# A CIN kernel's opening: table copies, queue assignments and a turn in two halves

## Chip, cores and metric

The kernel runs on one NeuronCore of a Trainium2 chip. The metric is the device time of one execution in microseconds (us). "PE" is TensorE, "DVE" VectorE, "ACT" ScalarE, "POOL" GpSimd and "SP" SyncE. Times inside an execution are counted from the start of the profiled span.

## The reference

Three layers of a compressed interaction network (CIN) over x of shape 1024 x 39 x 64 (batch, fields, embedding), all in float32:

```python
def _cin_layer(Xk, X0, W, b):
    O = W.shape[0]
    Hk, Fdim = (Xk.shape[1], X0.shape[1])
    Wr = W.reshape(O, Hk, Fdim)
    return jnp.einsum('bhe,bfe,ohf->boe', Xk, X0, Wr) + b[None, :, None]
X0 = sparse_embedding
Xk = X0
outs = []
for W, b in ((W0, b0), (W1, b1), (W2, b2)):
    Xk = _cin_layer(Xk, X0, W, b)
    outs.append(Xk.sum(axis=-1))
cin_output = jnp.concatenate(outs, axis=-1)
return cin_output @ fc_w.T + fc_b
```

W0 is 64 x 1521, W1 and W2 are 64 x 2496, fc_w is 1 x 192; the output is 1024 x 1.

## The kernel before

**The main loop.** Products of pairs of fields are formed once and multiplied by weights. The batch is cut into 32 blocks of 2048 columns (32 samples of 64). For each block, tables `r` (four tiles of 128 rows), and for each pair of blocks `u` and `v`, hold fields of x gathered row by row from DRAM, so that each elementwise product of two table tiles on DVE (L163, L165) covers 128 pairs of fields. PE multiplies each product tile by a weight tile `wa` in four quarters of 512 columns into PSUM `po` (L489). A pair of blocks has 13 products: six for each block and one, of `u` and `v`, that both share. ACT and DVE finish a block (L508, L514, L519), and at the end one row of PE matmuls makes the output.

**The tables' way.** `load(n)` (L117, L119) writes block n's x, fields first, into a DRAM tile `xd`: 312 KB in pieces of 256 B. There are three such tiles, for two blocks each, with one more row of ones behind each block's 39 fields. `gather_rows` (L124, L125) is an indirect DMA on POOL's queue: it fetches a tile's 128 rows by a list of row numbers (`lists`). For block 0 alone there are two smaller DRAM tiles `xh`, one for each half of its columns, so that its first gathers can start early: x goes there by ACT's queue (L204) and the ones by SP's (L201). `xd[0]` is filled for both blocks by two loads on POOL's queue, load(1) behind six of block 0's gathers and load(0) behind the last (L285, L288). `roll_half(0)` gathers `u` and `v`, `roll(1)` block 1's four tables.

**The head**, before the first matmul of the loop, makes the weights. In the order of PE's program:

- `spin` (L229): matmuls of zeros that only keep PE running; the tile `zeros` is set by DVE (L189). Two of them, then `small` (L296) from the copies of fcrow on POOL (L276), then two more.
- L316: W2, weighted by `fc2` (L299), into `pv`; L294: five small turns of fc rows; L331: twenty transposes of W0's two halves `w0s` into `pw`.
- DVE (L337, L344) and ACT (L345) make V2 (`v2`) from `pv`. After one spin, L386 and L392 multiply W1 by V2: `w1s` holds W1's lower and upper half of columns in two groups of 64 partitions, which arrive by SP's queue (L202) and ACT's (L208).
- The result T lies in `pt` (fields 0 to 31) and `pv` (the last seven). DVE and ACT copy it into `part` (L407, one half of the columns of each field by each) and `rest` (L401). PE then turns it: `turn_fields` (L412), eight transposes of rows 64.. into `pw[1]`, eight of rows 0.. into `pw[0]`, four of `rest` into `pt[0]`; and three spins.
- `untwine` (L373) copies from `pw` and `pt` into the tile `both`; `pairs` (set to zero on POOL, L214) receives sums of elements of `both` (`weight_rows`, L438 on DVE, L442 on ACT); PE turns a weight tile (L473), ACT copies it to `wa` (L474), and L489 begins.

Each engine executes its instructions in the order of the program, and each DMA queue belongs to the engine that issues it. A tile framework adds the waits: for data, for buffers, and for a DMA that takes over the completion semaphore of an earlier one, of which there are eight for SP and ACT together and eight for POOL. That last kind is why, before the change, ACT's issue of W1's upper half (L208) waits for W2's arrival, and its issue of `xh[1]` for that of fcrow.

Of the kernel before, what the change touches and what calls it, by code (L numbers as in the profile page):

```python
# [54 lines left out]
F32 = mybir.dt.float32  # L55
# [5 lines left out]
B, F, E, H = 1024, 39, 64, 64  # L61
FH = F * H
# [12 lines left out]
MM = 512  # L75
SUB = 1024
BLK = 2048
NA = 16
NR = F - 2 * NA
NW = 20  # L80
# [3 lines left out]
FT = F + 1  # L84
# [14 lines left out]
def cin_kernel(ctx: ExitStack, tc: tile.TileContext, x, w0t, b0, w1, b1, w2, b2, fc_w, fc_b, out):  # L99
    nc = tc.nc  # L100
# [10 lines left out]
    xd = [dram.tile([2 * FT, BLK], F32, name=f"xd{k}") for k in range(NTAB)]  # L111
    xh = [dram.tile([FT, SUB], F32, name=f"xh{k}") for k in range(2)]

    def bank(name):
        return psum.tile([128, MM], F32, name=name, tag="po")

    def load(n, engine=nc.sync):  # L117
        first = n % 2 * FT
        engine.dma_start(  # L119
            xd[n // 2 % NTAB][first : first + F].rearrange("f (b e) -> f b e", e=E),  # L120
            xv[:, n * BB : (n + 1) * BB, :],
        )

    def gather_rows(dst, table, k):  # L124
        nc.gpsimd.indirect_dma_start(  # L125
            dst, None, table, bass.IndirectOffsetOnAxis(ap=lists[:, k : k + 1], axis=0)
        )
# [21 lines left out]
    rt = [const.tile([128, 4, BLK], F32, name=f"r{k}") for k in range(2)]  # L149
# [3 lines left out]
    both = const.tile([128, F * FT], F32, name="both")  # L153
    pairs = const.tile([128, NCHUNK, 128], F32, name="pairs")
# [13 lines left out]
    prep = tc.tile_pool(name="prep", bufs=1)  # L168
    with prep as prep:
        w2s = prep.tile([128, FH // 2], F32, name="w2s")  # L170
        w1s = prep.tile([128, FH // 2], F32, name="w1s")
        w0s = prep.tile([128, NW * H], F32, name="w0s")
        part = prep.tile([128, NA, H], F32, name="part")
# [2 lines left out]
        fcrow2 = prep.tile([1, H, 2], F32, name="fcrow2")  # L176
        fc2 = prep.tile([128, H], F32, name="fc2")
        ones = prep.tile([16, 2, 128], F32, name="ones")
        zeros = prep.tile([128, MM // 2], F32, name="zeros")
        warm = prep.tile([1, 1], F32, name="warm")  # L180
        place = prep.tile([128, 1], I32, name="place")
        apart = prep.tile([128, 128], I32, name="apart")
# [3 lines left out]

        nc.vector.memset(zeros, 0.0)  # L189
        nc.vector.memset(ones, 1.0)  # L190
        nc.vector.memset(fc2, 0.0)
        nc.vector.memset(v2, 0.0)
        nc.vector.memset(warm, 0.0)

        w0v = w0t.rearrange("b a h -> b (a h)")
        nc.sync.dma_start(fcrow, fc_w)
        nc.scalar.dma_start(w2s, w2.rearrange("o (s n) -> (o s) n", s=2))
        for s, n in enumerate((NW, F - NW)):
            nc.scalar.dma_start(w0s[H * s : H * s + F, 0 : n * H], w0v[:, s * NW * H : (s * NW + n) * H])
        for k in range(2):  # L200
            nc.sync.dma_start(xh[k][F:FT].rearrange("r (p c) -> p r c", c=128), ones[0:8, 0:1])  # L201
        nc.sync.dma_start(w1s[0:H], w1[:, 0 : FH // 2])  # L202
        for k in range(2):
            nc.scalar.dma_start(  # L204
                xh[k][0:F].rearrange("f (b e) -> b f e", e=E), x[k * SB : (k + 1) * SB]
# [4 lines left out]
        for i in range(3):  # L210
            for k, by in enumerate((STEP[i + 1], BASE[i + 1], EXTRA[i + 1] - K)):
                nc.gpsimd.memset(shifts[:, k, i : i + 1], float(by))
        nc.gpsimd.iota(apart, pattern=[[1, 128]], base=0, channel_multiplier=-1)
        nc.gpsimd.memset(pairs, 0.0)  # L214
        bothv = both.rearrange("p (a b) -> p a b", b=FT)
        nc.gpsimd.memset(bothv[0:H, :, F], 0.0)
        nc.scalar.copy(warm, warm)


# [1 line left out]
        pt = [bank("pt") for _ in range(2)]  # L221
        idle = bank("idle")
        pw = [bank("pw") for _ in range(2)]
        small = bank("small")


        def spin(n=1):
            for _ in range(n):
                nc.tensor.matmul(idle[:, 0 : MM // 2], zeros[:, 0:128], zeros, start=True, stop=True)  # L229

        spin(2)


        tmp = prep.tile([128, 16], F32, name="tmp")
# [5 lines left out]
        def new():  # L240
            used[0] += 1
            return tmp[:, used[0] - 1 : used[0]]

        def step(x, at, by, out=None):

            out = new() if out is None else out
            nc.vector.tensor_scalar(out, x, at, by, ALU.is_ge, ALU.mult)
            return out
# [4 lines left out]
        row, f0, j, extra, t, half, q = new(), new(), new(), new(), new(), new(), new()  # L253
# [21 lines left out]
        for s in range(2):  # L275
            nc.gpsimd.tensor_copy(fcrow2[:, :, s], fcrow[:, 2 * H : 3 * H])  # L276

        for k in range(NTAB):
            nc.gpsimd.dma_start(xd[k][F::FT].rearrange("r (p c) -> p r c", c=128), ones)

        halves = [slice(0, SUB), slice(SUB, BLK)]
        for k, cols in enumerate(halves):
            for i in range(3):
                gather_rows(rt[0][:, i, cols], xh[k], i)
        load(1, nc.gpsimd)  # L285
        for k, cols in enumerate(halves):
            gather_rows(rt[0][:, 3, cols], xh[k], 3)
        load(0, nc.gpsimd)  # L288


        one = ones[0:1, 0, 0:1]
# [6 lines left out]
        )  # L298
        nc.vector.tensor_scalar(fc2[:, 0::32], mask, small[:, 0:1], None, ALU.mult)  # L299
        nc.vector.tensor_scalar(unit, apart, 0, None, ALU.is_equal)  # L300
        spin(2)


        step(row, HR, 1.0, half)
        fused(q, half, -float(HR), row, ALU.mult, ALU.add)
        nc.vector.tensor_tensor(field[4], q, step(q, F, -float(F)), ALU.add)
        nc.vector.tensor_tensor(field[4], field[4], step(q, 56, 11.0), ALU.add)

# [4 lines left out]
        for k in range(2):  # L313
            for u in range(4):
# [5 lines left out]
                    start=True,  # L320
                    stop=True,
# [6 lines left out]
        for s in range(2):  # L328
            for k in range(NW // 2):
                n = min(128, (F - NW * s) * H - k * 128)  # L330
# [33 lines left out]
        copies = (nc.vector.tensor_copy, nc.scalar.copy)  # L364
# [24 lines left out]
        for s in range(2):  # L389
            rows = slice(H * s, H * s + H)  # L390
            for k in range(2):
# [4 lines left out]
                    start=True,  # L396
                    stop=True,
                )
        for s, copy in enumerate(copies):
            at = slice(32 * s, 32 * s + 32)  # L400
# [1 line left out]
                rest[:, :, at],  # L402
                pv[s][H * s : H * s + H, 0 : 32 * NR].rearrange("b (a h) -> b a h", h=32),
            )
        for s, copy in enumerate(copies):
            at = slice(32 * s, 32 * s + 32)
            copy(part[:, :, at], pt[s].rearrange("b (a h) -> b a h", h=32))  # L407

        def turn_fields(to, src, rows, n):
            for a in range(0, n, 2):  # L410
                m = min(2, n - a)
                nc.tensor.transpose(  # L412
                    to[0 : m * H, a // 2 * FT : a // 2 * FT + FT],
                    src[rows, a : a + m, :].rearrange("b a h -> b (a h)"),
                    unit[rows, rows],
                )

        spin()
        for k in (1, 0):
            turn_fields(pw[k], part, slice(H * k, H * k + FT), NA)  # L420
        turn_fields(pt[0], rest, slice(0, FT), NR)
        for k in (1, 0):
            untwine(copies[k], 1, NA * k, NA, NA // 2, pw[k], FT)
# [133 lines left out]
    p = {}  # L557
# [14 lines left out]
    n, c = steps[3]  # L572
# [8 lines left out]
    for at, (n, c) in enumerate(steps[:-TAIL]):  # L581
# [17 lines left out]
        if at + AHEAD < len(steps):  # L599
            n, c = steps[at + AHEAD]  # L600
# [70 lines left out]
```

## Time and profile before

| | |
|---|---|
| five runs | 750.69, 751.57, 752.64, 753.55, 753.83 us; median 752.64 |
| the profiled execution | 751.6 us of its own; span 749.8 us |
| PE busy in the span | 741.3 us (99%), of which L489 722.5 us |
| DVE, ACT, POOL busy | 643.2, 164.2, 318.7 us |
| first L489 | 22.1 us |
| half clock of PE | about 20.5 to 23.9 us |
| DMA | 180.40 MB, mean 241 GB/s |

A row of the groups reads: line, engine, operation, output <- inputs, shapes, count, then busy us and mean ns of one, then the idle time of the engine just before these instructions and what ended most of it. An idle time that ends on "remote" or on an unknown queue has a releaser that the profile could not name. Matmul ends are modelled, not observed. A float32 matmul is two passes, so the 896 matmuls of the loop stand as x1792.

### The profile page before, as it was taken

To read this page: it belongs to the slowest core of one execution; us is meant where nothing else is said; L and a number is where in the kernel's file an instruction comes from. 1 tells how busy PE (TensorE), PEld (TensorE's weight loads), DVE (VectorE), ACT (ScalarE), POOL (GpSimd) and SP (SyncE) were. 2 spreads that over 40 slices of the span, in tenths; PEclk is the share of its full clock that TensorE was granted. 3 is DMA by queue.
4 is the path that set the end of the run, shared out by engine and by line. 5 is a ranking of instruction groups with operands and counts; after the bars stand their busy time and mean duration, and the time that the engine had idled before them with its cause. 6 is when DMAs were issued, how large, how long until landed. Compare 5 with 4: busy or idle time off the path is not lost.

```text
span 749.8 us, 5288 instructions
## 1 busy us (share of the span) xinstructions
PE 741.3 (99%) x1911; PEld 324.0 (43%) x1911; DVE 643.2 (86%) x509; ACT 164.2 (22%) x224; POOL 318.7 (43%) x198
## 2 busy tenths in 40 slices
PE   8899999999999999999999999999999999999998
PEld 4444444444444444444444444444444444444443
DVE  4989899888889888899888899888899888898885
ACT  2122212221212222112221212222112221212222
POOL 6568633436243263532436243263532436343100
PEclk9999999999999999999999999999999999999999
DMA  7789976865757876565866757776575855747400
GB/s 230 255 304 382 375 303 202 336 244 201 289 174 281 259 278 246 184 275 205 336 235 213 272 183 287 259 273 238 191 284 204 336 224 180 271 148 299 168 1 0
DMA packets 59050, 180.40 MB, mean 241 GB/s; under 512 B 37164, under 2 KB 37229, under 8 KB 39056
## 3 DMA queue, kind: packets, MB, share of 16 engines
q0 software_dynamic: 24512, 169.76, 59.9%
q1 hardware_dynamic: 32902, 8.64, 5.1%
q10 hardware_dynamic: 1610, 1.67, 0.8%
q8 instruction: 15, 0.25, 0.1%
q14 instruction: 11, 0.09, 0.0%
HBM read 179.98 MB, written 10.60 MB: 254 GB/s over the span
## 4 chain that ended last, share of the span: by engine, by line
PE 99%; ACT 0%; another core or an unknown queue 0%; DVE 0%; issue 0%; ACTq 0%
PE po L489 96%; PE idle L229 1%; PE pt L392 0%; PE pv L316 0%; PE pt L412 0%; PE pw L331 0%; PE tr L473 0%; PE pw L412 0%; ACT both L373 0%; DVE g L528 0%; DVE sums L530 0%; ACT zq L527 0%; ACT part L407 0%; PE pv L386 0%
## 5 line engine op out<-in xcount | busy, mean ns | idle before, releaser
L489 PE MATMUL po<-p,wa 128*128 128x512 f32 (+1 forms) x1792 | 722.5, 595 | 0.0
L163 DVE TENSOR_TENSOR p<-r 128x2048 f32<-128x2048 f32 (+2 forms) x196 | 434.7, 2246 | 85.8 <-PE po L489 81.8
L489 PEld LDWEIGHTS po<-p,wa 128*128 128x128 f32 (+1 forms) x1792 | 313.7, 190 | 405.1 <-issue 384.9
L125 POOL DMA_INDIRECT r<-xd,lists x124 | 246.6, 1989 | 354.9 <-DVE p L163 334.2
L508 ACT ACTIVATE z<-po,fc0s 64x512 f32<-64x512 f32 x124 | 84.7, 683 | 354.2 <-PE po L489 347.3
L502 ACT COPY g<-u 39x1024 f32<-39x1024 f32 x64 | 66.6, 1043 | 184.5 <-DVE sums L519 184.3
L514 DVE SCALAR_TENSOR_TENSOR g<-po,b0s,z 64x512 f32<-64x512 f32 x124 | 86.4, 734 | 0.0
L519 DVE TENSOR_REDUCE sums<-g 103x16 f32<-103x1024 f32 x62 | 75.6, 1220 | 2.1
L125 POOL DMA_INDIRECT u<-xd,lists x16 | 34.1, 2131 | 11.5 <-DVE p L163 6.9
L165 DVE TENSOR_TENSOR p<-u,v 128x2048 f32<-128x2048 f32 x16 | 36.5, 2284 | 0.0
L125 POOL DMA_INDIRECT v<-xd,lists x16 | 17.7, 1109 | 4.9 <-issue 4.9
L125 POOL DMA_INDIRECT r<-xh,lists x8 | 7.7, 963 | 6.6 <-DVE v L344 4.5
L229 PE MATMUL idle<-zeros 128*128 128x256 f32 x20 | 8.2, 538 | 1.2 <-DVE zeros L189 1.2
L528 DVE SCALAR_TENSOR_TENSOR g<-po,b0s,zq 64x512 f32<-64x512 f32 x4 | 3.0, 743 | 5.3 <-ACT zq L527 5.3
L119 POOL DMA_DIRECT2D xd<-in_x x6 | 6.3, 1070 | 0.0
L373 DVE COPY both<-pw 64x390 f32<-64x390 f32 (+1 forms) x4 | 2.1, 523 | 4.8 <-remote 4.7
L229 PEld LDWEIGHTS idle<-zeros 128*128 128x128 f32 x20 | 4.6, 259 | 3.6 <-issue 1.8
L473 PE MATMUL tr<-unit,pairs 128*128 128x128 f32 x7 | 2.1, 305 | 4.0 <-ACT pairs L442 4.0
L474 ACT COPY wa<-tr 128x128 f32<-128x128 f32 x7 | 1.9, 266 | 19.1 <-PE tr L473 19.1
L438 DVE TENSOR_TENSOR pairs<-both 128x6 f32<-128x6 f32 (+27 forms) x50 | 5.4, 178 | 0.3 <-DVE both L373 0.3
L527 ACT ACTIVATE zq<-po,fc0s 64x512 f32<-64x512 f32 x4 | 2.7, 684 | 10.2 <-PE po L489 10.2
L473 PEld LDWEIGHTS tr<-unit,pairs 128*128 128x128 f32 x7 | 1.1, 161 | 6.1 <-ACT pairs L442 4.3
(92 smaller groups left out, 46.4 us busy)
## 6 DMA issues: line engine op xcount, KB each, us to landing
xd<-in_x SPq DMA_DIRECT2D x26, 312.0 KB
r<-xd,lists POOLq DMA_INDIRECT x124
xd<-in_x POOLq DMA_DIRECT2D x6, 312.0 KB
w2s<-in_w ACTq DMA_DIRECT2D x1, 624.0 KB
w1s<-in_w SPq DMA_DIRECT2D x1, 312.0 KB
xh<-in_x ACTq DMA_DIRECT2D x2, 156.0 KB
w1s<-in_w ACTq DMA_DIRECT2D x1, 312.0 KB
u<-xd,lists POOLq DMA_INDIRECT x16
```

The source lines that it names most:

```text
L119: engine.dma_start(xd[n // 2 % NTAB][first : first + F].rearrange("f (b e) -> f b e", e=E), xv[:, n * BB : (n + 1) * BB, :],)
L125: nc.gpsimd.indirect_dma_start(dst, None, table, bass.IndirectOffsetOnAxis(ap=lists[:, k : k + 1], axis=0))
L163: nc.vector.tensor_tensor(p[:, cols], r[:, i, cols], r[:, k, cols], ALU.mult)
L165: nc.vector.tensor_tensor(p, ut[n // 2 % 2], vt[n // 2 % 2], ALU.mult)
L229: nc.tensor.matmul(idle[:, 0 : MM // 2], zeros[:, 0:128], zeros, start=True, stop=True)
L438: nc.vector.tensor_tensor(out, diagonal(a, b, sa, sb), diagonal(b, a, sb, sa), ALU.add)
L473: nc.tensor.transpose(tr[:, at], pairs[:, c], unit)
L489: nc.tensor.matmul(po[n + h][m], wa[w, c, :], p[w, bass.ts(m, MM)], start=c == opens[n + h], stop=c == closes[n + h],)
L502: nc.scalar.copy(gt[H : H + F], ut[n // 2 % 2][h : h + F, bass.ts(m, SUB)])
L508: nc.scalar.activation(z[m // 2][:, bass.ts(m % 2, MM)], po[n][m][H:128], AF.Identity, bias=fc0s[H:128])
L514: nc.vector.scalar_tensor_tensor(gt[0:H, at], po[n][m][0:H], b0s, z[m // 2][:, at], ALU.add, ALU.mult)
L519: nc.vector.tensor_reduce(sums[:, b_at : b_at + SB], gt.rearrange("p (b e) -> p b e", e=E), AX.X, ALU.add)
```

## The change

Five edits, all ahead of the main loop.

1. `spin` reads a built-in constant of 1.0, broadcast, so the tile `zeros` and its memset go. There are three spins at first instead of two, and behind `small` one of 256 and one of 128 columns instead of two of 256.
2. The ones of `xh` are written by POOL's queue, ahead of `apart`, instead of SP's; the memsets of `pairs` and of a column of `both` move on POOL from ahead of the mask and the fcrow copies to behind them.
3. W1's lower half still goes by SP's queue, but waits for a memset of one of its columns that DVE executes behind the lists' work; W1's upper half stays where it was on ACT's queue.
4. Block 0's rows in `xd[0]` are copied from `xh[0]` and `xh[1]` (39 rows of 4 KB each) by SP's queue instead of loaded from x by POOL's; load(1) goes by SP's queue behind them.
5. T is copied to `part` in two halves of the fields by each of DVE and ACT, and turned in the order rows 64.., rows 0.. for the first half of the fields, then again for the second.

With this, completion semaphores are dealt out anew: ACT's issue of W1's upper half waits for none, and that of `xh[1]` for W2's arrival. The gathers of block 0 stand one behind the other on POOL, with no load between.

```diff
-        zeros = prep.tile([128, MM // 2], F32, name="zeros")
...
-        nc.vector.memset(zeros, 0.0)
         nc.vector.memset(ones, 1.0)
...
-        for k in range(2):
-            nc.sync.dma_start(xh[k][F:FT].rearrange("r (p c) -> p r c", c=128), ones[0:8, 0:1])
-        nc.sync.dma_start(w1s[0:H], w1[:, 0 : FH // 2])
...
+        for k in range(2):
+            nc.gpsimd.dma_start(xh[k][F:FT].rearrange("r (p c) -> p r c", c=128), ones[0:8, 0:1])
         nc.gpsimd.iota(apart, pattern=[[1, 128]], base=0, channel_multiplier=-1)
-        nc.gpsimd.memset(pairs, 0.0)
-        bothv = both.rearrange("p (a b) -> p a b", b=FT)
-        nc.gpsimd.memset(bothv[0:H, :, F], 0.0)
...
-        def spin(n=1):
+        def spin(n=1, cols=MM // 2):
             for _ in range(n):
-                nc.tensor.matmul(idle[:, 0 : MM // 2], zeros[:, 0:128], zeros, start=True, stop=True)
-
-        spin(2)
+                nc.tensor.matmul(
+                    idle[:, 0:cols],
+                    nc.const_aps.tensor(1.0, (128, 128), F32),
+                    nc.const_aps.tensor(1.0, (128, cols), F32),
+                    start=True,
+                    stop=True,
+                )
+
+        spin(3)
...
+        nc.gpsimd.memset(pairs, 0.0)
+        bothv = both.rearrange("p (a b) -> p a b", b=FT)
+        nc.gpsimd.memset(bothv[0:H, :, F], 0.0)
         for k in range(NTAB):
             nc.gpsimd.dma_start(xd[k][F::FT].rearrange("r (p c) -> p r c", c=128), ones)
-
-        halves = [slice(0, SUB), slice(SUB, BLK)]
-        for k, cols in enumerate(halves):
-            for i in range(3):
-                gather_rows(rt[0][:, i, cols], xh[k], i)
-        load(1, nc.gpsimd)
-        for k, cols in enumerate(halves):
-            gather_rows(rt[0][:, 3, cols], xh[k], 3)
-        load(0, nc.gpsimd)
...
-        spin(2)
+        spin()
+        spin(1, MM // 4)
...
+        nc.vector.memset(w1s[0:H, 0:1], 0.0)
+        nc.sync.dma_start(w1s[0:H], w1[:, 0 : FH // 2])
+
+        halves = [slice(0, SUB), slice(SUB, BLK)]
+        for k, cols in enumerate(halves):
+            for i in range(3):
+                gather_rows(rt[0][:, i, cols], xh[k], i)
+        for k, cols in enumerate(halves):
+            gather_rows(rt[0][:, 3, cols], xh[k], 3)
+            nc.sync.dma_start(xd[0][0:F, cols], xh[k][0:F])
+        load(1)
...
-        for s, copy in enumerate(copies):
-            at = slice(32 * s, 32 * s + 32)
-            copy(part[:, :, at], pt[s].rearrange("b (a h) -> b a h", h=32))
-
-        def turn_fields(to, src, rows, n):
-            for a in range(0, n, 2):
+        for q in range(2):
+            for s, copy in enumerate(copies):
+                fields = slice(q * NA // 2, (q + 1) * NA // 2)
+                copy(
+                    part[:, fields, 32 * s : 32 * s + 32],
+                    pt[s].rearrange("b (a h) -> b a h", h=32)[:, fields],
+                )
+
+        def turn_fields(to, src, rows, n, start=0):
+            for a in range(start, n, 2):
...
-        for k in (1, 0):
-            turn_fields(pw[k], part, slice(H * k, H * k + FT), NA)
+        for q in range(2):
+            for k in (1, 0):
+                rows = slice(H * k, H * k + FT)
+                turn_fields(pw[k], part, rows, (q + 1) * NA // 2, q * NA // 2)
```

More of the change, by code (lines that the diff above doesn't have):

```diff
@@ L198, in cin_kernel @@
         for s, n in enumerate((NW, F - NW)):
-            nc.scalar.dma_start(w0s[H * s : H * s + F, 0 : n * H], w0v[:, s * NW * H : (s * NW + n) * H])
-        for k in range(2):
-            nc.sync.dma_start(xh[k][F:FT].rearrange("r (p c) -> p r c", c=128), ones[0:8, 0:1])
-        nc.sync.dma_start(w1s[0:H], w1[:, 0 : FH // 2])
+            nc.scalar.dma_start(
+                w0s[H * s : H * s + F, 0 : n * H], w0v[:, s * NW * H : (s * NW + n) * H]
+            )
         for k in range(2):
@@ L404, in cin_kernel @@
             )
-        for s, copy in enumerate(copies):
-            at = slice(32 * s, 32 * s + 32)
-            copy(part[:, :, at], pt[s].rearrange("b (a h) -> b a h", h=32))
-        def turn_fields(to, src, rows, n):
-            for a in range(0, n, 2):
+        for q in range(2):
[4 more added lines that the diff above has]
+                    pt[s].rearrange("b (a h) -> b a h", h=32)[:, fields],
+                )
+        def turn_fields(to, src, rows, n, start=0):
+            for a in range(start, n, 2):
                 m = min(2, n - a)
```

## The prediction

> **What bounds the kernel now.** I read the page first, then the chain of waits, then the timeline of the first 50 us, then the table by stage. The page says that TensorE is never without work once the main loop runs:
>
> ```profile
> PE 741.3 (99%) x1911; PEld 324.0 (43%) x1911; DVE 643.2 (86%) x509; ACT 164.2 (22%) x224; POOL 318.7 (43%) x198
> ...
> PE 99%; ACT 0%; another core or an unknown queue 0%; DVE 0%; issue 0%; ACTq 0%
> ...
> L489 PE MATMUL po<-p,wa 128*128 128x512 f32 (+1 forms) x1792 | 722.5, 595 | 0.0
> ```
>
> The last line is the main matmul: 722.5 us busy, 0.0 us idle before it. Nothing in the diff touches L489, its operands or its count, so the change can move only what lies before the first of them (22.1 us), or starve them later. The chain of waits shows what that head is made of (start us, us, what):
>
> ```profile
> 9.86 0.63 PE idle L229 x2
> 10.49 0.54 PE pv L386 x2
> ...
> 14.33 0.97 PE pw L412 x16
> 15.29 1.31 PE pt L412 x4
> ...
> 17.49 2.03 another core or an unknown queue
> ...
> 20.98 0.45 PE tr L473
> 21.43 0.85 PE idle L229 x2
> 22.28 1.71 PE po L489 x2
> ```
>
> W2 by fc (L316), W0's turns (L331), W1 by V2 (L386, L392), the copies of T (L407), T's turns (L412), copies into `both` (L373), weight rows (L438), one turn (L473), first matmul. The 2.03 us of an unknown queue are put in their place by the timeline (start, us, engine line, then the idle time ahead and what ended it):
>
> ```profile
> 16.63 0.86 ACT L373 COPY both<-pw 64x320 f32<-64x320 f32 x2 [2.35 <-PE pt L412]
> 18.81 0.99 DVE L373 COPY both<-pw 64x320 f32<-64x320 f32 x2 [4.74 <-remote]
> 19.54 0.55 ACT L373 COPY both<-pt 64x160 f32<-64x160 f32 x2 [2.05 <-remote]
> 20.75 1.28 DVE L163 TENSOR_TENSOR p<-r 128x512 f32<-128x512 f32 x2
> 28.19 2.15 POOL L125 DMA_INDIRECT u<-xd,lists  x1 [6.88 <-DVE p L163]
> 44.06 2.29 DVE L163 TENSOR_TENSOR p<-r 128x2048 f32<-128x2048 f32 x1 [2.92 <-DMA r<-xd,lists]
> ```
>
> The program order has these three copies wait for TensorE (the third also for DVE), so "remote" is T's turns whose results arrive later than the profile draws their ends: 16.6, 18.8 and 19.5 for turns drawn as over by 15.5. The last two rows are the supply of later tables. The table by stage adds the clock (the last three figures of a row are PE's granted clock, the DMA share and GB/s):
>
> ```profile
> 20.00:21.00 1.00, 0.02 (x1) 0.05 (x2) 0.88 (x7) 0.30 (x2) 1.00 (x2) 0.73 1.03 410
> 21.00:22.00 1.00, 1.00 (x3) 0.78 (x4) 1.00 (x3) 0.52 (x4) 0.32 (x1) 0.50 1.09 345
> 22.00:23.00 1.00, 1.00 (x3) 0.47 (x3) 1.00 (x8) 0.27 (x2) 0.00 (x0) 0.50 0.95 373
> ```
>
> PE is at half clock from about 20.5 to 23.9.
>
> **What the Trainium skill says.** "TensorE: Matmul & The Clock Gate", Part 1: a free-running window of about 3.4 us without activity halves the clock. The trace agrees: PE stands still from 17.0 to 21.0 and 0.50 follows. The same page, Part 4, puts a turn on PE at some 275 ns in one kernel and says that turns do not count as activity. Here (18.8 - 14.3) / 16 = 0.28 us for each of T's turns, but W0's twenty go from 8.67 to 10.5, 0.1 us each, so the figure is no constant. "Perfetto Trace Analysis", Per-instruction lifecycle, Tensor Engine Instruction: a matmul's drawn end is estimated and its semaphore comes only when PSUM acknowledges; the late copies agree. "DMA: Bandwidth & Descriptors", Issuing engines are not separate DMA queues: moving a transfer to another engine saves only issue time. DMA shares of 0.85 to 1.19 in every microsecond from 2 to 9 agree: the start is full whoever issues.
>
> **The change part by part.** Times are against this execution: span 749.8, own time 751.6, 1.0 under the median of 752.64.
>
> *Spins and ones.* PE's first spins read a built-in constant, so they no longer wait for the zeros (1.14) and start near 0.8. Three pairs cost 0.59 + 5 x 0.43 = 2.7 us, to 3.5. `small` (L296, at 3.19 now) waits for the POOL copies of fcrow, and ahead of these come two DMA issues (0.50 to 0.76 us each, from the three rows of L279), while the memset of pairs (0.85) and of both (0.18) goes behind. They end now at 3.1; then at 1.27 + 1.2 + 0.24 + 0.8 = 3.5. So `small` starts at 3.5 to 3.7, 0.4 later; the spin behind it is 4 passes now (4 x 0.43 + 0.16 = 1.9) and 1.4 then. L316 starts at 5.6 to 5.9 against 5.71: zero, bounds -0.1 and +0.2. The moved memset ends near 4.6; the first weight rows want it at 20.1.
>
> *W1 together.* The lower half leaves SP at 2.07 now. Then it waits for a memset that DVE does behind L307's work, 0.5 us later than now since it follows `small`: issue at 5.7. The upper half on ACT loses its wait (issued 5.17, after 2.3 us of standing for w2s) and goes at 2.9; now xh's second half stands there instead, for the same w2s, to 5.1. Same bytes, same 16 engines, busy until 10 now. Behind SP's W1 stand the two table copies and the load of block 1; behind ACT's xh stands the table load of ACT, first needed at 8.8. The need: L386 starts at 10.42, when the spin before it (9.79 + 0.63) lets it, with V2 ready at 9.6. Left to move at 5.7 are about 0.16 + 0.64 + 0.16 MB; at the 240 to 390 GB/s of 3 to 9 us, 2.5 to 4 us: W1 lands between 8.5 and 10. I take no cost. If that cover fails, L386 and all behind it slip one for one. W1 together gains nothing either, because the spin and not W1 holds L386.
>
> *First block's gathers.* xh's ones go by POOL, its x earlier by W1's absence: gathers start some 1 us before 9.36. Two copies (156 KB, 4 KB rows) and the load of block 1 (312 KB in 256 B pieces, the kind that lowers GB/s to 84 to 228 in 8 to 10 us) now run beside them: estimated 1 + 1.7 us of DMA time. DVE asks for the first two tables at 20.75 and for later ones every 1 to 2 us; by the trace's completion records the second table is in at 16.2. Slack 4 us against 2.7 added and 1 gained: zero.
>
> *Block 1.* POOL loses two DMA issues (1.08 + 1.05, and 0.3 each). `u` need no longer wait for a load issued at 20.26: it can go at about 18.5 instead of 28.19, and with it v and block 1's four tables, 9 us sooner. Today DVE stands 2.92 us at 44.06 for them; its product is ready at 46.35, and PE, counted from 22.28 in matmuls of 0.86 us, takes it at about 47.5. So 1.1 us of slack becomes 4 or more; in this execution worth zero, in one with slower DMAs a little.
>
> *T by halves.* Each copy of 0.59 (ACT) and 0.69 (DVE) becomes two; by the fixed part of small copies (0.15 to 0.2) a half costs about 0.37, so two cost 0.1 to 0.15 more, beside PE. The first eight turns start when ACT's first half is out: 13.69 + 0.37 = 14.06 instead of 14.28, 0.2 to 0.3 earlier; the other half is out at 14.4, while those turn. Sixteen turns at 0.28 and four at 0.19 as now: pw0 at 18.5, pt at 19.2. ACT's wait for pw1 moves from eight turns to twelve (17.4), copies done 18.3, before pt: hidden. Gain 0.25 us on the path; bounds +0.2 (switching rows four times instead of once costs something) and -3.5 (the turns run at W0's 0.1 us).
>
> *Half clock.* What is gained is gained inside the half-clock stretch, so 0.25 becomes 0.15 to 0.25. The sum: 0.0 - 0.2 + 0 = **-0.2**, and -0.1 for block 1's tables in the runs above this execution: 752.64 - 0.3 = **752.3 us**.
>
> **Rivals.** 0.3% (2.3 us) is about what a measurement of this kernel can tell from no change.
>
> (A) *The head barely moves*, as worked out: 750.8 to 754. For it: 0.0 idle at L489, and four parts of five off the chain. Chance 0.67.
>
> (B) *T's turns speed up.* With rows 64.. and 0.. alternating by fours they overlap as W0's seem to. 20 x 0.1 = 2.0 us instead of 5.2: up to -3.2; and PE then idles under 3.4 us, which saves the half clock (1.8 us of matmuls and 1.2 of turn and spin at half speed: 1.5). Halfway, -3: **749.6**. Against: the sixteen turns now also change rows once, and were slow. Chance 0.16 for faster.
>
> (C) *W1's lower half comes late*, the slower side. Its SP transfer issued at 2.07 now is complete, by the trace's completion records, at 8.2: 6.2 us. From 5.7 the same makes 11.9, 1.6 us after L386's 10.3; if it also shares with ACT's half and xh, 13: +2.7, **755.3**. It decides from a landing past 10.3 and is measurable from 12.6. Against: most of the 6.2 us was queueing behind w2s and w0s, which are gone by then. Chance 0.17 for slower, with other mishaps of the queue.
>
> That the change doesn't do what it says is small: the instruction order of the changed kernel has the second wait after eight turns, and `u` waits for SP's load.
>
> **Numbers.** Range 750.0 to 754.9: A whole (the five runs alone spread over 3 us), the nearer half of B and of C. Faster 0.16, same 0.67, slower 0.17.
>
> **What would show it.** Right: first L489 at 21.7 to 22.2; L386 within 0.3 of 10.4; pw0's DVE copy at 18.3 to 18.8; `u` near 18.5; no DVE wait for a DMA near 44; L489 idle 0.0. Wrong: a gap before L386 (C); the copies from pw at 16 to 17 and no 0.50 in the clock (B); DVE waiting for r in 20 to 27, which would mean that SP's transfers cost the gathers over 4 us.

## The result, and the profile after

The changed kernel takes 755.08 us (median of 27 runs, 753.02 to 763.41) against 752.45 for the kernel before (48 runs); the ratio of the times is 1.0038, 95% interval [1.0026, 1.005]. It is 0.38% slower, where 752.3 was predicted. The profiled execution has a span of 753.0 us. In its page the loop is as it was, and the lost time lies ahead of it (the last figures of the lower lines are busy us, mean ns, then idle time before and what ended it):

```profile
PE 741.8 (99%) x1913; PEld 324.9 (43%) x1913; DVE 643.2 (85%) x510; ACT 164.3 (22%) x225; POOL 322.8 (43%) x198
...
PE 97%; another core or an unknown queue 1%; DVE 1%; DMA 1%; POOL 0%; issue 0%; ACT 0%; DVEq 0%
...
L504 PE MATMUL po<-p,wa 128*128 128x512 f32 (+1 forms) x1792 | 722.6, 595 | 0.0
...
L382 DVE COPY both<-pw 64x390 f32<-64x390 f32 (+1 forms) x4 | 2.1, 524 | 7.1 <-remote 7.1
```

L504 (L489 before) still has 0.0 us idle ahead of it and 722.6 us of work. The chain of the page now holds 1% each of DMA, DVE and an unknown queue. In order of time (start us, us, what) that chain shows where:

```profile
5.84 5.34 DMA w1s<-in_w
...
11.31 0.70 PE pv L395 x2
...
14.24 0.76 DVE part L417 x2
15.00 7.03 another core or an unknown queue
...
22.06 0.48 DVE both L382
...
24.05 0.45 PE tr L488
24.50 0.85 PE idle L224 x2
25.35 1.71 PE po L504 x2
```

The first matmul of the loop starts at 25.14 in the timeline, 3.07 us later than the 22.07 of before. By stages: W1 by V2 (L395, was L386) starts at 11.31 for 10.42, +0.89, of which 0.52 is the wait for W1; from there to T's turn 3.55 us for 3.91, -0.36; from the turn (14.86) to DVE's copy out of `pw[0]` (22.06) 7.20 us for 4.48, **+2.72**; from there to the first matmul -0.18. Nearly all of the loss stands in the piece of 7.03 us whose releaser the profile could not name. The timeline of the changed kernel has this around it (start, us, engine line, then idle before and what ended it):

```profile
14.86 0.73 PE L425 MATMUL pw<-unit,part 40*128 40x40 f32 x16
15.43 0.39 PE L425 MATMUL pt<-unit,rest 40*128 40x40 f32 x4
15.60 0.94 POOL L125 DMA_INDIRECT r<-xh,lists  x1 [0.30 <-issue]
16.85 0.93 POOL L125 DMA_INDIRECT r<-xh,lists  x1 [0.31 <-issue]
18.09 0.94 POOL L125 DMA_INDIRECT r<-xh,lists  x1 [0.30 <-issue]
18.50 0.86 ACT L382 COPY both<-pw 64x320 f32<-64x320 f32 x2 [3.52 <-PE idle L224]
19.33 0.94 POOL L125 DMA_INDIRECT r<-xh,lists  x1 [0.30 <-issue]
22.06 0.99 DVE L382 COPY both<-pw 64x320 f32<-64x320 f32 x2 [7.06 <-remote]
22.11 0.55 ACT L382 COPY both<-pt 64x160 f32<-64x160 f32 x2 [2.75 <-remote]
...
25.14 1.91 PE L504 MATMUL po<-p,wa 128*128 128x512 f32 x2
...
26.90 1.01 POOL L125 DMA_INDIRECT u<-xd,lists  x1 [6.63 <-DVE p L163]
```

T's twenty turns are drawn from 14.86 to 15.82, and only a spin (14.23, 0.70 us) stands on PE's queue just ahead of them; yet what waits for them starts 3.6 to 7.3 us after their beginning. The trace also records when PE raises its own semaphore: for the turns into `pw` at 18.48 and 22.03, for those into `pt` at 22.09, and for the three spins behind them, drawn as over at 17.32, at 22.17. So DVE and ACT start as soon as they are told; it is PE's signal that is late. Whether PE also did the work late, the trace does not show, since the ends that it draws are modelled. Meanwhile POOL issues one gather after another, every 1.24 us. In the kernel before, the timeline has a longer step at the same place:

```profile
15.73 0.94 POOL L125 DMA_INDIRECT r<-xh,lists  x1 [0.30 <-issue]
...
16.67 1.08 POOL L119 DMA_DIRECT2D xd<-in_x  x1
18.05 0.98 POOL L125 DMA_INDIRECT r<-xh,lists  x1 [0.30 <-issue]
```

There load(1) stands between the sixth and the seventh gather, 2.32 us apart. The experiments below come back to this step.

PE's longer standstill also lengthens the half clock: in the table by stage PE's clock (third figure from the end) is 0.50 from 21 to 27. Of the loop itself the first 2.1 us run at half clock, against 1.8 before.

```profile
22.00:23.00 1.00, 0.00 (x0) 0.00 (x0) 0.93 (x2) 0.54 (x2) 0.00 (x0) 0.50 1.04 421
26.00:27.00 1.00, 1.00 (x3) 0.38 (x2) 1.00 (x4) 0.00 (x0) 0.10 (x1) 0.50 0.10 41
```

### The profile page after: what moved, and what is told of

It is laid out like the page before. It is cut to its first block, busy times and chain, and to the rows that moved or that the text cites. A ratio compares the mean times of both kernels' runs of the same rounds, so it can differ in the third digit from the quotient of the medians.

```text
span 753.0 us, 5294 instructions
## 1 busy us (share of the span) xinstructions
PE 741.8 (99%) x1913; PEld 324.9 (43%) x1913; DVE 643.2 (85%) x510; ACT 164.3 (22%) x225; POOL 322.8 (43%) x198
## 4 chain that ended last, share of the span: by engine, by line
PE 97%; another core or an unknown queue 1%; DVE 1%; DMA 1%; POOL 0%; issue 0%; ACT 0%; DVEq 0%
PE po L504 96%; DMA w1s<-in_w 1%; PE pt L401 0%; POOL xh L210 0%; PE tr L488 0%; DVE both L382 0%; PE idle L224 0%; PE pv L395 0%; DVE part L417 0%; DVE g L543 0%; DVE pairs L453 0%; DVE sums L545 0%; ACT zq L542 0%; PE small L291 0%
## 5 line engine op out<-in xcount | busy, mean ns | idle before, releaser
L504 PE MATMUL po<-p,wa 128*128 128x512 f32 (+1 forms) x1792 | 722.6, 595 | 0.0
L504 PEld LDWEIGHTS po<-p,wa 128*128 128x128 f32 (+1 forms) x1792 | 313.8, 190 | 405.1 <-issue 384.5
L125 POOL DMA_INDIRECT r<-xd,lists x124 | 250.4, 2019 | 354.4 <-DVE p L163 330.4
L125 POOL DMA_INDIRECT v<-xd,lists x16 | 20.2, 1263 | 4.9 <-issue 4.9
L224 PE MATMUL idle<-const-float32-1.0 128*128 128x256 f32 (+1 forms) x22 | 8.6, 526 | 0.8 <-PEq L673 0.8
L224 PEld LDWEIGHTS idle<-const-float32-1.0 128*128 128x128 f32 x22 | 5.3, 266 | 3.3 <-issue 2.6
L489 ACT COPY wa<-tr 128x128 f32<-128x128 f32 x7 | 1.9, 266 | 19.3 <-PE tr L488 19.3
L119 POOL DMA_DIRECT2D xd<-in_x x4 | 4.1, 1063 | 0.0
```

The lines of the kernel that those rows point to most:

```text
L119: engine.dma_start(xd[n // 2 % NTAB][first : first + F].rearrange("f (b e) -> f b e", e=E), xv[:, n * BB : (n + 1) * BB, :],)
L125: nc.gpsimd.indirect_dma_start(dst, None, table, bass.IndirectOffsetOnAxis(ap=lists[:, k : k + 1], axis=0))
L224: nc.tensor.matmul(idle[:, 0:cols], nc.const_aps.tensor(1.0, (128, 128), F32), nc.const_aps.tensor(1.0, (128, cols), F32), start=True, sto ...
L504: nc.tensor.matmul(po[n + h][m], wa[w, c, :], p[w, bass.ts(m, MM)], start=c == opens[n + h], stop=c == closes[n + h],)
```

## First experiments: which edit

"Median" is that of the kernel named; the kernel before, run beside it, had 752.1 to 752.8 in every comparison. Lines differ a little between kernels; the copies out of `pw` and `pt` are always those called `both<-pw` and `both<-pt`.

**u_load**: edit 4 undone, both loads on POOL as before.

```diff
-        for k, cols in enumerate(halves):
-            gather_rows(rt[0][:, 3, cols], xh[k], 3)
-            nc.sync.dma_start(xd[0][0:F, cols], xh[k][0:F])
-        load(1)
+        load(1, nc.gpsimd)
+        for k, cols in enumerate(halves):
+            gather_rows(rt[0][:, 3, cols], xh[k], 3)
+        load(0, nc.gpsimd)
```

> The changed kernel with edit 4 alone undone: block 0's and block 1's x go into xd[0] by POOL's queue again, load(1) behind six gathers and load(0) behind the last. Theory 1 (the transfers that SP now issues between 9.6 and 13 us run in the stretch in which T is turned, and hold up the turns' results): the DVE copy out of pw[0] starts at 18.8 to 19.5 instead of 22.06, the first main matmul comes near 22.5 instead of 25.14, the time is 752.3 to 753.2. Theory 2 (the order of T's turns by halves is itself slow): nothing moves, copy near 22, time near 755. Theory 3 (W1's late lower half alone): near 755, less what W1 gains.

752.56, ratio 1.0002 [0.999, 1.0015]: the loss is gone, with all other edits in. DVE copies out of `pw[0]` 3.2 us after the turn begins (16.02, 19.21), and the first main matmul is at 22.10. W1's wait is still there, 0.75 us ahead of L395 at 11.94, and costs nothing that can be measured.

**u_turn**: edit 5 undone (T copied and turned as before).

```diff
-        for q in range(2):
-            for k in (1, 0):
-                rows = slice(H * k, H * k + FT)
-                turn_fields(pw[k], part, rows, (q + 1) * NA // 2, q * NA // 2)
+        for k in (1, 0):
+            turn_fields(pw[k], part, slice(H * k, H * k + FT), NA)
```

> The changed kernel with edit 5 alone undone: T copied whole, and turned eight by eight. Theory 1: still slow, copy out of pw[0] near 21 to 22, time 754.5 to 755.5. Theory 2: copy near 19.5, time near 752.5.

755.08, ratio 1.0047 [1.0023, 1.0072]. In this profile it is W0's turns and T itself that came late (ACT's copy out of `pw` at 15.30 after 5.21 us on "remote"), and T's turns, at 21.80, only 1.5 us. So the halves are not the cause, and what is late is whatever PE finishes in that stretch.

**u_w1**: the wait of edit 3 taken away, W1's lower half issued on SP ahead of everything else.

```diff
-        nc.vector.memset(w1s[0:H, 0:1], 0.0)
-        nc.sync.dma_start(w1s[0:H], w1[:, 0 : FH // 2])
...
+        nc.sync.dma_start(w1s[0:H], w1[:, 0 : FH // 2])
         for k in range(2):
             nc.scalar.dma_start(
```

> The changed kernel with edit 3 alone undone: W1's lower half is issued by SP early, without the wait on DVE's memset. All theories: L386's counterpart starts at 10.6 to 10.8 instead of 11.31 (its spin then ends last), so 0.5 to 0.8 us come back ahead of T. Theory 1: the late turns remain, time 754.3 to 754.8. Theory 3: W1 is the cause of all, time near 752.5.

755.23, ratio 1.0037 [1.0021, 1.0053]: nothing is gained. Alone this doesn't clear W1, since in its profile the second half of W0 arrives late instead (PE waits 1.04 us for that DMA, until 10.41) and W1 by V2 starts at 12.41, later than the 11.31 of the changed kernel. What clears W1 is u_load, which has W1's wait and no loss.

**gate**: six gathers of block 0, and POOL's later work, held until DVE has copied out of `pw[0]`; the copies and load(1) stay on SP.

```diff
+        gate = prep.tile([128, 1], F32, name="gate")
+        nc.gpsimd.tensor_copy(gate[H : H + 1], bothv[H : H + 1, 0, 0:1])
+        gather_rows(rt[0][:, 2, halves[0]], xh[0], 2)
...
```

> The changed kernel with six of block 0's eight gathers, and all later ones, held back on POOL until DVE has copied out of pw[0]; the two first gathers and SP's transfers stay where they are. It asks whether DMA traffic as such holds up the turns. If yes: the copy out of pw[0] starts 2 to 4 us after the first turn (at 17 to 19 us) instead of 7.2; block 0's later tables then come late (six half gathers of about 1.2 us each behind 18 us) and DVE waits for them, so the time may be anything from 751 to 758. If traffic has no part in it: the copy stays near 22 and the time goes up by the late tables, 758 or more.

753.96, ratio 1.0017 [1.0008, 1.0026]. The turn's results come 0.7 us after it begins (15.08, 15.81), the first main matmul at 18.86; then DVE waits for tables (3.80 at 23.74). So twenty turns need no 5 us: with few gathers about, they are over in one (PE raises its semaphore for the last of them at 16.03).

## Second experiments: copies, load(1), or its place

From gate I read that DMA traffic holds up PE's results, and edit 4 adds traffic. The two halves of edit 4 were taken alone.

**load1_sp**: load(1) on SP, called ahead of the last two gathers, block 0 loaded on POOL as before. **copies_sp**: the reverse, load(1) back on POOL behind six gathers.

```diff
 load1_sp: block 0's copies replaced
-            nc.sync.dma_start(xd[0][0:F, cols], xh[k][0:F])
+        load(0, nc.gpsimd)
 copies_sp: load(1) moved back, behind six gathers
-        load(1)
+        load(1, nc.gpsimd)
```

> The change with block 0's copy put back on GpSimd's queue behind all eight gathers (x to xd as before), load(1) still on SyncE, free of the gathers. Theory 1 (any transfer that joins the eight gathers ahead of T's turn holds up PE's results; load(1) is 312 KB of the 624 KB): about half of the loss, 753.6 to 754.2, DVE's copy out of pw[0] at 20.3 to 21. Theory 2 (it is load(1), whose many small packets run from 12.3 to 26): all of the loss, 754.7 to 755.3, copy at 21.5 to 22.5. Theory 3 (it is block 0's copies, which start first): none, 752.3 to 752.9, copy at 18.5 to 19.5.

> The other half: block 0's two copies (156 KB each) on SyncE as changed, load(1) back on GpSimd's queue behind six gathers. Theory 1 (the sum of the traffic counts): 753.6 to 754.2. Theory 2 (load(1)): no loss, 752.3 to 752.9, copy out of pw[0] at 18.5 to 19.5. Theory 3 (the copies): all of the loss, 754.7 to 755.3, copy at 21.5 to 22.5.

load1_sp 754.75, ratio 1.0033 [1.0021, 1.0046]; copies_sp 752.78, 1.0012 [1.0003, 1.0022]. The loss goes with load(1). I took this for its packets on SP ("theory 2"). But two things change with load(1): it comes to SP, and it leaves POOL.

**no_gate** leaves SP out: both loads on POOL, but behind all eight gathers (what follows on POOL is put behind T's turn in the program; the queue's order stays).

```diff
+        load(1, nc.gpsimd)      # behind the eighth gather
+        load(0, nc.gpsimd)
```

> u_load's order of gathers, both loads behind them, and the instructions that follow on GpSimd's queue (u, v, block 1's tables) put into the program behind T's turn in place of ahead of it; no gate. The queues hold the same instructions in nearly the same order. If the place in the program is what freed the turn: copies within 1 us of the turn, 749.5 to 751.5. If the order or the gate did: copies 2.3 to 4 after it, 752.2 to 753.

754.60, ratio 1.0035 [1.0022, 1.0048]: all of the loss is there with no transfer of blocks 0 and 1 on SP. I had expected at most 753. Its timeline:

```profile
17.82 0.94 POOL L125 DMA_INDIRECT r<-xh,lists  x1 [0.30 <-issue]
18.80 0.86 ACT L377 COPY both<-pw 64x320 f32<-64x320 f32 x2 [3.36 <-PE idle L224]
19.07 0.94 POOL L125 DMA_INDIRECT r<-xh,lists  x1 [0.30 <-issue]
20.01 2.11 POOL L119 DMA_DIRECT2D xd<-in_x  x2
20.24 0.99 DVE L377 COPY both<-pw 64x320 f32<-64x320 f32 x2 [4.83 <-remote]
21.66 0.55 ACT L377 COPY both<-pt 64x160 f32<-64x160 f32 x2 [2.00 <-remote]
```

The last result of the turn (15.31) is in use at 21.66, 6.3 us later; where load(1) breaks the row it takes 3.9 to 5.2 us (before, u_load, copies_sp, order_only). The profiled execution of load1_sp doesn't show its loss as clearly: there it takes 5.3 us (14.82, 20.15), in an execution of 753.87, its third fastest of nine.

**pause** parts the break from the transfer: the changed kernel, load(1) and the copies on SP, with a memset of a scratch tile on POOL between the sixth and the seventh gather.

```diff
+        pause = prep.tile([128, 1792], F32, name="pause")
+        nc.gpsimd.memset(pause, 0.0)
         for k, cols in enumerate(halves):
             gather_rows(rt[0][:, 3, cols], xh[k], 3)
```

> The changed kernel, load(1) and the copies on SyncE as changed, with a memset of a scratch tile (128 x 1792, estimated at 1.7 from the 0.84 of the memset of pairs, 896 wide) on GpSimd between the sixth and the seventh gather: a break in the issue of gathers with no transfer in it. If the break is what lets the turn's results through: last copy out of pt at 19.3 to 20.3, 752.2 to 753.2. If load(1)'s traffic on SyncE beside the gathers is what holds them up: last copy at 21.5 to 22.5 as in the changed kernel, 754.7 to 755.5.

752.22, ratio to the kernel before 0.9992 [0.9982, 1.0002]: one memset of 1.6 us gives the time back, while SP moves what it moved. The time came as the theory of the break had it, the place did not. In its profile the gathers begin earlier (8.73), so that W0's results are the ones caught, and ACT's copy of them starts in the break:

```profile
15.10 0.93 POOL L125 DMA_INDIRECT r<-xh,lists  x1 [0.30 <-issue]
16.03 1.61 POOL L317 MEMSET pause<- 128x1792 f32 x1
17.52 0.94 ACT L387 COPY both<-pw 64x390 f32<-64x390 f32 x2 [7.34 <-remote]
17.81 0.94 POOL L125 DMA_INDIRECT r<-xh,lists  x1 [0.16 <-issue]
...
23.93 1.13 PE L509 MATMUL po<-p,wa 128*128 128x512 f32 x2
```

So the last copy out of `pt` comes at 21.15, not by 20.3, and the loop starts at 23.93: 1.2 us earlier than in the changed kernel, but still 1.9 later than before. The span is 750.9 us, 2.1 under that of the changed kernel. The rest is about what the clock gives: PE is back at full clock at 23.3, ahead of the loop, where the changed kernel's loop loses about 1.0 us (an estimate: half of its 2.1 us at half clock). Whether other executions of pause divide their gain in the same way is not shown.

The kernels with six gathers or more in a row, by what stands behind the sixth:

| kernel | from sixth to seventh gather | median | ratio to before |
|---|---|---|---|
| before | load(1), 2.3 us | 752.1 to 752.8 | 1 |
| u_load | load(1), 2.3 | 752.56 | 1.0002 |
| copies_sp | load(1), 2.3 | 752.78 | 1.0012 |
| order_only | load(1), 2.3 | 752.96 | 1.0009 |
| pause | memset, 2.7 | 752.22 | 0.9992 |
| changed kernel | 1.24 | 755.08 | 1.0038 |
| u_turn | 1.24 | 755.08 | 1.0047 |
| u_w1 | 1.25 | 755.23 | 1.0037 |
| load1_sp | 1.25 | 754.75 | 1.0033 |
| no_gate | 1.24 | 754.60 | 1.0035 |
| hold2 | 1.3 | 755.24 | 1.0042 |
| hold3_old | 1.3 | 754.64 | 1.0034 |

(order_only, hold2 and hold3_old are told below; before's own row gives its medians in the six comparisons.) No median lies between 753.0 and 754.6. In the profiled executions the loop starts at 22.1 to 22.6 us with load(1) in the row and at 24.1 to 27.4 without a break; pause (23.9) and load1_sp (22.7) lie in between. hold3, told below too, is the exception: 1.3 us at that place and no loss.

## Third experiments: what holds the results, and can it be used

**tiny6** and **plain6** part the issue of gathers from their bytes.

```diff
 tiny6: six more gathers, of 16 columns, ahead; the eight real ones behind part
+            gather_rows(scrap[:, i], short[i % 2], i % 3)
 plain6: six gathers replaced by plain copies on SP
+                    nc.sync.dma_start(rt[0][32 * u : 32 * u + 32, i, cols], xh[k][0:32])
```

> The opposite: six extra gathers of 64 bytes per partition into a scrap tile (48 KB in all) are issued by GpSimd at the place of the first six, from about 9 to 17, and all eight real ones come behind part. So the issue stays in the turn's stretch and the traffic leaves it. Theory a (issue): copies out of pw 2.5 to 7 after the turn begins. Theory b (traffic): 0.7 to 1.2. The tables come some 9 late by design, so the PE stalls then and the time itself tells nothing (rounds 0).

> Leaves out the gather of fields 0 to 2 of block 0: in the place of those six gathers SyncE moves plain rows 0 to 31 of xh, four times each, into the same tables (24 transfers of 128 KB, the same 3 MB in 4 KB packets), and GpSimd issues nothing between 9 and the gate behind part. So the traffic into SBUF stays in the turn's stretch and GpSimd's issue leaves it. Theory a (issue): copies out of pw 0.7 to 1.2 after the turn begins. Theory b (traffic into SBUF): 2.5 to 7 after it. The time itself tells nothing (rounds 0).

Each was executed once, for its trace, and neither holds anything up. tiny6, with POOL issuing gathers through the turn (14.81 on):

```profile
15.26 0.94 POOL L125 DMA_INDIRECT scrap<-xh,lists  x1 [0.30 <-issue]
15.59 0.86 ACT L371 COPY both<-pw 64x320 f32<-64x320 f32 x2 [0.64 <-PE pw L434]
```

plain6, with SP's copies filling the DMA engines (share 0.96, second figure from the end; the turn begins at 14.98):

```profile
15.00:16.00 1.00, 1.00 (x22) 0.95 (x22) 0.23 (x1) 0.29 (x1) 0.40 (x1) 1.00 0.96 217
```

```profile
15.71 0.86 ACT L371 COPY both<-pw 64x320 f32<-64x320 f32 x2 [0.96 <-issue]
```

So in these two executions neither issue alone nor bytes alone held the results. That it takes both is likely, but one execution each doesn't prove it, as hold3 below lets results through beside full gathers too.

**hold6, hold5, hold4, hold3, hold2**: both loads on POOL behind all gathers, and 2, 3, 4, 5 or 6 gathers ahead of a POOL copy that waits for `part`, the rest behind it (and all that follows on POOL behind that); **hold3_old** is hold3 with the gathers in the old order, and **order_only** has hold3's order (fields 0 and 1 of both halves first) with load(1) at its old place and no gate.

```diff
+        gate = prep.tile([128, 1], F32, name="gate")
+        nc.gpsimd.tensor_copy(gate, part[:, NA - 1, 0:1])
         ...                                        # hold5: the last five gathers, then
+        load(1, nc.gpsimd)
+        load(0, nc.gpsimd)
```

> The change with nothing of block 0 or 1 on SyncE, two gathers (first half of fields 0 and 1) ahead, and the other six and both loads on GpSimd's queue behind DVE's last copy into part (about 14.2), so that their first packets come at about 15.3. If gather traffic in the stretch from 13 to 16 is what holds up the turns: copies out of pw within 1 us of the turn, at 15.3 to 16, first main matmul at 18.0 to 19.0, 3.0 to 4.0 earlier than before; DVE then waits for r where the gate kernel's did (3.8 at 23.7) by 1 to 2 us less than there, as the tables start 1.6 earlier and nothing of SyncE's runs beside them: 750.5 to 751.8 in all. If the first packets already hold up the copies out of pw (the issue takes less than 1 us), first main matmul at 19.5 to 21, 751 to 752.3. If the results are late for another reason, 752.3 to 753.

> The same with three gathers ahead and five behind. The third gather's packets run to about 15 by the pace of the before kernel (some 1.7 us each from 10.5 on). If the gathers' traffic holds up PE's results only while it saturates the queues, copies out of pw at 15.5 to 16.5, first main matmul at 18.3 to 19.5, and the last table 1.7 us earlier than with two ahead, so DVE's waits for r are under 1 us: 749.3 to 750.8. If three gathers already hold up the turn, copies at 17 to 18.5, first main matmul at 20.5 to 22: 751.5 to 752.7.

> Four gathers ahead of the turn, four behind DVE's last copy into part (hold5 had three and five: its turn's copies came at 15.3, its first main matmul at 18.36, and DVE then waited 2.4 for r, the PE 3.1). GpSimd stood idle for 2.3 before hold5's gate, and a gather is issued every 1.25, so the last tables come 1.25 earlier. Theory a (packets in flight do not hold up PE's results, gathers being issued during the turn do): copies out of pw at 15.2 to 15.8, first main matmul at 18.2 to 18.8, DVE's wait for r at 0.8 to 1.6 in place of 2.4: 751.3 to 752.4. Theory b (the amount in flight counts): copies at 16.5 to 18.5, first main matmul at 20 to 22: 752 to 753.2.

> Five gathers ahead, three behind. The fifth is issued at about 13.6 to 14.6, so it ends as the turn begins. Theory a: copies out of pw still within 1.2 of the turn (15.3 to 16), first main matmul at 18.3 to 19, DVE's wait for r under 0.5: 750.3 to 751.7. Theory b: copies at 17.5 to 19, first main matmul at 21 to 22.3, no wait for r: 752.3 to 753.2.

> Six gathers ahead of the gate, two behind: the sixth is issued at about 16, after part is copied, so the gate holds nothing back. If the amount issued by the turn decides (five or fewer): copies still within 1 us, 750.3 to 751.5, DVE's wait for r under 1.2. If the wait itself decides, which then comes after the turn's results are due: copies 2.3 to 4 after the turn, 752.2 to 753.2.

> hold3 with the old order of gathers (fields 0 to 2 of the first half, then of the second). If GpSimd's wait on part is what freed the turn: copies within 1 us, first main matmul at 18.3 to 21 (a table of the second half may now come last), 750.5 to 752.3. If the order did: copies 2.3 to 4 after the turn, 752.2 to 753.2.

> The changed kernel with both loads back on GpSimd's queue (as in u_load) and the eight gathers in hold3's order, fields 0 and 1 of both halves first; no gate. If the order is what freed the turn: copies out of pw within 1 us of the turn, first main matmul at 18.3 to 19.5, 749.5 to 751.2. If the gate or the place did: copies 2.3 to 4 after the turn as in u_load, 752.2 to 753.

**early_load**: order_only with load(1) between the fourth and the fifth gather.

```diff
-        load(1, nc.gpsimd)      # behind the sixth gather
+        load(1, nc.gpsimd)      # behind the fourth
```

> order_only with load(1) between the fourth and the fifth gather in place of the sixth and the seventh, so that the break of some 1.4 in the gathers' issue falls at 14.9 to 16.3, where the turn is. If the break lets the results through: copies out of pw at 15.6 to 16.8, first main matmul at 18.5 to 19.8, tables as in order_only, so DVE waits for r by up to 1.5: 750.3 to 751.8. If the break has nothing to do with it: copies at 18 to 20, 752.5 to 753.5.

hold2 and hold3_old, where the gate came too late to make a break (1.3 us between gathers), lost as the changed kernel did (hold3_old 754.64, 1.0034 [1.0024, 1.0044]), which neither of my forecasts for them allowed; order_only (1.0009 [1.0001, 1.0017]) did not, nor did its order free the turn: 3.8 us from turn to DVE's copy. The others had the turn's first results in use 0.7 to 0.8 us after it began:

| kernel | first main matmul | DVE's longest wait for r of block 0 | median | ratio |
|---|---|---|---|---|
| before | 22.1 | none | 752.1 to 752.8 | 1 |
| hold6 | 18.6 | 4.9 | 755.38 | 1.0045 [1.0032, 1.0058] |
| hold5 | 18.4 | 2.4 | 753.20 | 1.001 [1.0002, 1.0019] |
| hold4 | 19.0 | 2.3 | 752.27 | 1.0009 [0.9997, 1.0021] |
| hold3 | 18.6 | 1.2 | 751.18 | 0.9998 [0.9984, 1.0011] |
| early_load | 18.8 | 3.1 | 752.69 | 0.9998 [0.9987, 1.0009] |

The loop starts 3.1 to 3.7 us earlier, much as expected, and none is faster than the kernel before by what can be measured (hold3's median is 0.9 us under that of the kernel beside it, inside its interval). The times that I had forecast for hold6, hold5 and early_load, at most 750.8 to 751.8, were missed. The time is given back to the tables. In early_load:

```profile
14.60 1.09 POOL L119 DMA_DIRECT2D xd<-in_x  x1
15.71 0.86 ACT L385 COPY both<-pw 64x320 f32<-64x320 f32 x2 [0.67 <-PE pw L428]
15.99 0.99 POOL L125 DMA_INDIRECT r<-xh,lists  x1 [0.30 <-issue]
18.53 1.66 POOL L125 DMA_INDIRECT r<-xh,lists  x1 [0.30 <-issue]
22.96 1.23 DVE L163 TENSOR_TENSOR p<-r 128x1024 f32<-128x1024 f32 x1 [3.10 <-DMA r<-xh,lists]
```

The break falls on the turn, its results pass at once, and DVE then stands 3.10 us for a table. In hold3 the wait for block 0 is 1.2, but its load(1) is issued behind all gathers, and DVE waits 4.65 us at 46.11 for block 1's tables. A kernel with hold3's start and an earlier load(1) was not run.

**What stays open.** Why PE's signal is held is not settled. Long holds were seen only beside a row of full gathers, and a break in the row lets the results through. In five of the seven kernels without a break the last copy out of `pt` starts 1.5 to 1.9 us after the issue of the row's last gather has ended (in load1_sp 0.1 us after it; in u_turn T itself was late). But a short row holds too: in gate and hold6, two gathers hold one of W0's results for 2.0 and 1.6 us past its drawn end, and in hold5 three hold both, for 2.3 and 2.7 us. And hold3 has its results beside a row without a break:

```profile
14.79 0.94 POOL L125 DMA_INDIRECT r<-xh,lists  x1 [0.30 <-issue]
14.85 0.72 PE L430 MATMUL pw<-unit,part 40*128 40x40 f32 x16
15.58 0.86 ACT L372 COPY both<-pw 64x320 f32<-64x320 f32 x2 [0.60 <-PE pw L430]
```

PE raises its semaphore at 15.56, 15.62 and 15.81 there, as the turns are drawn. In hold3_old, with the same steps, another order and a start 0.5 us later, the results were held (turn at 15.12, last copy at 21.59). Nor do the traces say which of the results in flight is caught: T's turns in most, W0's in u_turn and pause.

## Why the prediction was wrong, point by point

- *First block's gathers* is the step that failed. It set the transfers moved to SP (2.7 us of DMA time) against DVE's slack for tables (4 us) and got zero. DVE indeed did not wait for r in 20 to 27. But the step asked only what the transfer adds where it goes, and not what it had done where it stood: between the sixth and the seventh gather it let PE's results out. Its worth: 752.22 (pause) against 755.08, 2.9 us by the medians. Nor did the gathers start some 1 us before 9.36, as the step had it: the first is issued at 10.46. But u_load has it at 10.66 and loses nothing. That the gathers then stand one behind the other, with no load between, was known from the change; no term of the sum priced it. The Trainium skill's "DMA: Bandwidth & Descriptors" (Issuing engines are not separate DMA queues), on which I leaned, counts only the issue time of such a move, 1.08 us here to be saved; measured, moving load(1) cost 2.3 us (755.08 against 752.78 for copies_sp). None of the signs of being wrong that I had listed names results that are held.
- *T by halves* took 4.5 us from turn to copy as the pace of the turns, 0.28 us each "as now". It was a wait: with the row broken at the turn (early_load) PE raises its semaphore for the last of the twenty at 15.94, 0.95 us after the first begins. The part that I credited to the halves, an earlier turn, came: 3.55 us from W1 by V2 to the turn for 3.91 (-0.36; predicted -0.25).
- *W1 together* was to land between 8.5 and 10. The chain has it at 11.18, 5.34 us after issue, and L395 waits 0.52 us for it. The step had counted on the 240 to 390 GB/s of 3 to 9 us; read by the microsecond these were 207 to 391 before the change, and after it the trace has 180 to 251 from 5 to 10 us. The sign of rival (C) was right and the landing past its threshold of 10.3; but its mechanism is a fifth of the 2.6 us at most, and u_load, with a wait of 0.75 us for W1, has no loss. Rival (C)'s 755.3 met the number for another reason.
- *Spins and ones*: L325 starts at 6.02 against 5.71, +0.3, just past the bound of +0.2; `small` at 3.93 was predicted for 3.5 to 3.7.
- *Block 1*: `u` was gathered at 26.90, not 18.5, since load(1) on SP, issued at 12.29, ended by the trace's completion records only at 26.05 (the profile then names a product of DVE, over at 26.86, as what released `u`). DVE's wait of 2.92 at 44 went all the same, and was worth nothing, as predicted: L504 has 0.0 us of idle time in either case.
- *Half clock*: the step reckoned with one stretch; it became twice as long, two of 3.4 us (20.4 to 27.2). The first falls into PE's idle time, the second slows the loop's first matmuls for 2.1 us instead of 1.8, so that this cost little (0.15 us, an estimate: half of the difference).
- Rival (B), faster turns worth 3 us, has its effect (results in 0.7 us) but by other means, and its gain is spent on DVE's waits for tables, which the rival did not price.

## What to carry to other kernels

When a transfer is moved off a queue, price what it leaves behind as well: it may have been the only pause in a row of gathers beside which another engine's results were held. When copies wait on "remote" for instructions drawn as long over, treat that time as a wait with a cause to be found, not as the pace of the instructions. And before a stage is sped up, see what is late next: here 3.7 us earlier at the loop's start bought nothing, because the tables came no earlier.

## What the runs showed of the hardware

- PE's semaphore for a row of short transposes was raised 2.9 to 6.4 us after their drawn end, and that for the spins behind them 4.9 us after theirs, while GpSimd issued indirect gathers of 128 rows of 4 KB every 1.24 us (the changed kernel). The results were in use 0.7 to 0.8 us after the turn's start with a break there (early_load), with plain copies at a DMA share of 0.96 (plain6), with gathers of 64 bytes (tiny6), and once beside full gathers (hold3).
- A gather's issue on GpSimd, 0.94 us in most rows, took 1.66 (early_load at 18.53), 2.37 (hold5 at 17.36) and 5.15 us (the changed kernel's `v` at 28.21) where DVE was at its products and weight rows; the trace shows the coincidence alone.
- A load of 312 KB in 256 B pieces on SyncE took 13.8 us beside the gathers.
